# Kernel1's products with W, cut into stretches of 256 tokens

## The chip, the cores and the metric

The kernel runs on one core of one Trainium2 chip. The time is the device time of one execution in microseconds (us), and a kernel's time is the median over its runs. The core has five engines with instruction queues of their own: TensorE (PE in the profile; its weight loads are listed as PEld), VectorE (DVE), ScalarE (ACT), GpSimd (POOL) and SyncE (SP). Each works through its queue in order, and semaphores make one wait for another. The program has about 93,000 instructions, all laid out before it runs: there is no branch.

## The reference

Two layers over x, 16 batches of 1024 tokens by 256 features, all in float32. The first is a Nyström attention with 16 heads of 16 features and 64 landmarks:

```
Q = Q / sqrt(16)
Q_l, K_l = means of Q and K over groups of 16 tokens       # 64 landmarks
kernel1 = softmax(Q @ K_l^T)                               # tokens x landmarks
kernel2 = softmax(Q_l @ K_l^T)                             # landmarks x landmarks
kernel3 = softmax(Q_l @ K^T)                               # landmarks x tokens
SV  = (kernel1 @ iterative_inv(kernel2)) @ (kernel3 @ V)
out = SV @ w_proj
x   = x + layernorm(out)
```

iterative_inv is six steps of a Newton-like iteration with 64x64 matrices. The second layer normalizes x, computes for each batch the reconstruction loss of eight small experts, picks the expert with the least loss, and adds the layer norm of a base projection plus that expert's adapter.

## The kernel before, in words

**Four streams.** Each batch goes through four stages, and a Stream object runs each stage over all batches: a (norm, Q, K, V, kernel3 and its product with V, called u), p (kernel2 and its inverse, ending in W = inverse times u), c (kernel1, its product with W, the projection and the residual), and d1 with d2 (the experts). They are staggered: while d works on batch b, c works on b + 1, p on b + 2 and a on b + 3, roughly.

**The scheduler.** A stage is a generator. Before each step it yields `go(name, follows, parts)`: the step's name, the steps that must be over, and its parts: `mm(us, mode, n)` is TensorE work of estimated time us, in an array mode ("full", "r32", "c32", "q64"), of n instructions, and takes one PSUM slot; `ew(engine, us, behind, mark)` is work of another engine, where "free" gives a slot back. The loop at L1105 takes among the streams' next steps the one with the least key: for a step that starts on TensorE, the estimated idle time that it would put on TensorE (counted as zero up to 0.15 us), then the stream's progress less 0.1 if the step has the mode that TensorE is in; a step without TensorE goes first once its inputs are nearly there. The estimate in `tried` keeps a clock for each engine, four PSUM slots handed out in turn, 0.09 us for a change of mode, and instructions that arrive in blocks of 256, one every 3.4 us at most (BLOCK, FETCH; `run`). The order so chosen is the order of the instructions in every engine's queue.

**PSUM.** There is one pool, ps2, with four buffers of two banks each (L58). `two_banks` and `one_bank` are two names for the same allocation (L74 to L78): every tile, large or small, takes one of the four in turn, so a new tile waits until the tile allocated four places before it has been read.

**Stage c around the change.** A batch's tokens are handled in two windows n of 512. In each window, for each half c of the heads (8 heads, 4 pairs):

- `before_weights` and `weights` (L728): scores in transposed form, landmarks of a pair of heads on the partitions and 512 tokens along the row, less each token's maximum; two psct tiles; ScalarE takes the exponential into two e tiles (e1).
- the maxima of the next window (`max_of`, L686: two psc tiles, one VectorE reduction each), or in the last window the residual of the window before.
- `before_weighted` and `weighted` (L754): the product with W. The 512 tokens are four groups j of 128; for each j, each pair p and each group g of 32 tokens, 32 columns of e are the weights, and the 34 columns of w_bd (two heads by 16 features and a column of ones) stream through. These are 64 matmuls in the code and 128 in the profile, where a float32 matmul here is two; four run side by side, on four groups of 32 columns of the array. They fill a tile psv. The column of ones gives the softmax's denominators: VectorE takes their reciprocal (rec) and multiplies (svn).

After both halves of the heads, `turned_sv` (L779) transposes svn on TensorE (ptsv), ScalarE copies it (svt), and `projected` (L804) multiplies by w_proj (po).

The steps of other streams that appear below: ph and pr (experts' hidden layer and reconstruction, L879 and L911; VectorE evicts pr as df, L919, ScalarE squares it, L922), pq and pv (Q, K and V, L309 and L330), psm and psc of stage a (kernel3, L378 and L402), put (its product with V, L441), pm (transposed maxima, L723), rrow (a small step of the inverse's start, L584), and the inverse's 64x64 products, all at L533 (pkv, psq, pb, pvi).

Of the kernel before, what the change touches and what calls it, by code (L numbers as in the profile page):

```python
# [8 lines left out]
F32 = mybir.dt.float32  # L9
I32 = mybir.dt.int32  # L10
AF = mybir.ActivationFunctionType
ALU = mybir.AluOpType
# [3 lines left out]
P = 128  # L16
# [6 lines left out]
def kernel(  # L23
# [17 lines left out]
    nc = tc.nc  # L41
    NB, N, D = x.shape
    NT = N // P
    H, HD, M = 16, 16, 64
    G = N // M
    NC = D // P
    HC = H // NC
    NP = H // 2
    PC = NP // NC
    E, _, R = wa_down.shape  # L50
# [6 lines left out]
    small = ctx.enter_context(tc.tile_pool(name="small", bufs=2))  # L57
    ps2 = ctx.enter_context(tc.tile_pool(name="ps2", bufs=4, space=PSUM))  # L58

    def last(ap, n):  # L60

        return ap.unsqueeze(len(ap.shape)).to_broadcast([*ap.shape, n])
# [8 lines left out]
    def rows32(p):  # L71
        return slice(32 * p, 32 * p + 32)

    def two_banks(shape, name):  # L74
        return ps2.tile(shape, F32, tag="ps2", name=name)

    def one_bank(shape, name):
        return ps2.tile(shape, F32, tag="ps2", name=name)  # L78

    def buf4k(tag, shape, name, bufs=2):  # L80

        return work.tile(shape, F32, tag=tag, name=name, bufs=bufs)
# [70 lines left out]
    for c in range(NC):  # L153
        for r in range(2):
            j = 2 * c + r
# [49 lines left out]
    def mm(us, mode, n, bank="ps2"):  # L205
        return ("pe", us, mode, bank, n)

    def ew(engine, us, behind=-1, mark=""):
        return (engine, us, behind, mark)

    def go(name, follows, *parts):
        return name, follows, parts
# [457 lines left out]
    def stage_c(b):  # L670
# [5 lines left out]
        def before_max(n, t0):  # L676
            return go(
                ("c", b, "max", n, t0),
                first,
                mm(0.5, "r32", 32),  # L680
                mm(0.5, "r32", 32),
                ew("dve", 1.13, 1, "free"),
                ew("dve", 1.13, 1, "free"),
            )

        def max_of(n, t0):  # L686

            mx = maxima[n]
            psc = [two_banks([P, 2, 2, NC, P], f"psc1_{b}_{n}_{t0}_{g}") for g in range(PC // 2)]
            for c in range(NC):  # L690
                for t in range(2):
                    cols = slice((4 * n + t0 + t) * P, (4 * n + t0 + t + 1) * P)
                    for p in range(PC):
                        nc.tensor.matmul(  # L694
                            psc[p // 2][:, p % 2, t, c, :],
                            lhsT=qt[rows32(p), c, cols],
                            rhs=bd[rows32(p), NC + c, :, :].rearrange("f r l -> f (r l)"),
                            start=True,
                            stop=True,
                        )  # L700
            for g in range(PC // 2):
                nc.vector.tensor_reduce(  # L702
                    mx[:, t0 : t0 + 2, 64 * g : 64 * g + 64].rearrange("x t (p j) -> x p t j", p=2)[
                        :, :, :, 0 : 2 * NC
                    ],
                    psc[g].rearrange("x p t c (r l) -> x p t (c r) l", r=2),
                    X,
                    ALU.max,
                )

        def before_rows(n):
            return go(
                ("c", b, "mt", n),
                [("c", b, "max", n, t0) for t0 in range(0, 4, 2)],
                mm(0.44, "full", 8),
                ew("act", 0.5, -1, "free"),
            )
# [10 lines left out]
        def weights(n, c, mt):  # L728

            psc = [two_banks([P, 2, 512], f"psct_{b}_{n}_{c}_{g}") for g in range(PC // 2)]  # L730
            for p in range(PC):
                nc.tensor.matmul(  # L732
                    psc[p // 2][:, p % 2, :],
                    lhsT=bd[rows32(p), NC + c, :, :].rearrange("f r l -> f (r l)"),
                    rhs=qt[rows32(p), c, n * 512 : (n + 1) * 512],
                    start=True,
                    stop=False,
                )
            for p in range(PC):
                nc.tensor.matmul(  # L740
                    psc[p // 2][:, p % 2, :],
                    lhsT=minus_max[rows32(p), c, :, :].rearrange("f r l -> f (r l)"),
                    rhs=mt[rows32(p), :],
                    start=False,
                    stop=True,
                )
            es = []
            for g in range(PC // 2):
                e = buf4k("e1", [P, 2, 512], f"e1_{b}_{n}_{c}_{g}")
                nc.scalar.activation(e, psc[g], AF.Exp)  # L750
                es.append(e)
            return es

        def weighted(n, c, es, svn):  # L754

            psv = two_banks([P, 2, 512], f"psv_{b}_{n}_{c}")
            for j in range(4):
                for p in range(PC):
                    col = (j % 2) * PC * 2 * (HD + 1) + p * 2 * (HD + 1)
                    for g in range(4):  # L760
                        nc.tensor.matmul(  # L761
                            psv[rows32(g), j // 2, col : col + 2 * (HD + 1)],
                            lhsT=es[p // 2][:, p % 2, j * P + 32 * g : j * P + 32 * g + 32],
                            rhs=w_bd[:, c * PC + p].rearrange("x r d -> x (r d)"),
                            start=True,
                            stop=True,
                        )
            by_head = psv[:, :, 0 : 2 * H * (HD + 1) // 2].rearrange("x k (h d) -> x k h d", d=HD + 1)
            rec = small.tile([P, 2, H], F32, tag="rec", name=f"rec_{b}_{n}_{c}")
            nc.vector.reciprocal(rec, by_head[:, :, :, HD])  # L770
            for k in range(2):
                nc.vector.tensor_tensor(
                    svn[:, 2 * k : 2 * k + 2, c * P : (c + 1) * P].rearrange("x j (h d) -> x j h d", d=HD),
                    by_head[:, k, :, 0:HD].rearrange("x (j h) d -> x j h d", j=2),
                    last(rec[:, k, :], HD).rearrange("x (j h) d -> x j h d", j=2),
                    ALU.mult,
                )

        def turned_sv(n, svn):  # L779
            pt = two_banks([P, NC, 512], f"ptsv_{b}_{n}")  # L780
            for j in range(4):
                for c in range(NC):
                    nc.tensor.transpose(pt[:, c, j * P : (j + 1) * P], svn[:, j, c * P : (c + 1) * P], ident)
            nc.scalar.copy(svt[n], pt)  # L784

        def before_weights(n, c):
            return go(
                ("c", b, "e1", n, c),
                [("c", b, "mt", n)],
                mm(0.9, "r32", 16),  # L790
                mm(0.9, "r32", 16),
                ew("act", 0.93, 1, "free"),
                ew("act", 0.93, 1, "free"),
            )

        def before_weighted(n, c):
            return go(
                ("c", b, "sv", n, c),
                [("c", b, "e1", n, c), ("p", b, "end")],
                mm(1.15, "c32", 256),  # L800
                ew("dve", 0.95, -1, "free"),
            )

        def projected(n):  # L804
# [13 lines left out]
        def added(n, y, stats):  # L818
            res = live[b]["x1"][:, 4 * n : 4 * n + 4, :]
            yield from add_normalized(b, "c", n, y, stats, res, res)  # L820
# [10 lines left out]
        for n in range(NW):  # L831
            for c in range(NC):
                yield before_weights(n, c)
                es = weights(n, c, mt)
                if n + 1 < NW:
                    yield before_max(n + 1, 2 * c)
                    max_of(n + 1, 2 * c)
                elif c == 0:
                    yield from added(n - 1, *po)
                yield before_weighted(n, c)  # L840
                if c == 0:
                    svn = buf4k("yc", [P, 4, D], f"svn_{b}_{n}")
                weighted(n, c, es, svn)
            if n + 1 < NW:
                yield before_rows(n + 1)
                mt = max_rows(n + 1)
            yield go(
                ("c", b, "svt", n),
                [("c", b, "sv", n, c) for c in range(NC)],
                mm(0.88, "full", 16),  # L850
                ew("act", 0.93, -1, "free"),
            )
            svt[n] = work.tile([P, NC, 512], F32, tag="svt", name=f"svt_{b}_{n}", bufs=1)
            turned_sv(n, svn)
            po = yield from projected(n)
# [249 lines left out]
    with tc.manual_schedule(engines={mybir.EngineType.PE, mybir.EngineType.Activation, mybir.EngineType.DVE, mybir.EngineType.Pool}):  # L1105
        while any(s.takes for s in streams):
# [13 lines left out]
            _, s, at = best  # L1120
# [43 lines left out]
```

## Time and profile before

| what | value |
|---|---|
| median of 14 runs | 2582.27 us (2572.36 to 2592.65) |
| the profiled execution | 2588.31 us; span from first to last instruction 2586.5 us |
| mean granted TensorE clock in it | 0.961 |
| PE / PEld / DVE / ACT / POOL busy | 2310.1 / 1509.7 / 1544.0 / 1253.6 / 277.4 us |
| psv matmuls (L761) | 8192, 94.8 us busy |
| reciprocals (L770) | 64 of 128x32, 350 ns each |
| multiplications (L772) | 128 of 128x256, 420 ns each |

In the profile's lines, "out<-in" are the program's tile names, then the shapes as partitions x elements, then the count. In a group's line the numbers behind the bar are the busy time in us, the mean duration in ns and the idle time of the engine just ahead of these instructions, with what ended it. A line of the waits reads: who, for whom, us in total, times, the longest. "issue" means that the engine waited for nothing that the profile shows. The chain is the work that ended last, followed back from the last instruction.

### The profile page before, as it was taken

The numbers are of one execution on the slowest core, as the hardware profiler recorded it, in microseconds if no ns is written. First come the engines' busy times: TensorE is split into PE (matmuls) and PEld (weight loads), VectorE is DVE, ScalarE is ACT, GpSimd is POOL, SyncE is SP. The second block draws the span as 40 slices with busy tenths as digits, with TensorE's granted clock in tenths as the row PEclk, the third lists the DMA queues.
The fourth block names the chain that finished last, engine by engine and source line by source line (L and its number), as shares of the span: only waits on it lengthen the run. The fifth ranks groups of instructions, "written<-read, shape, count | busy, mean of one in ns | idle before, by whom it ended". The sixth has DMA issues, their size and how long they took to land.

```text
span 2586.5 us, 93024 instructions
## 1 busy us (share of the span) xinstructions
PE 2310.1 (89%) x42930; PEld 1509.7 (58%) x42930; DVE 1544.0 (60%) x3242; ACT 1253.6 (48%) x2147; POOL 277.4 (11%) x372
## 2 busy tenths in 40 slices
PE   6998988989999899898989899998998989998975
PEld 3666556565655656556565655656566565655543
DVE  5547465575666656665585665647566575664654
ACT  1344554545546355453645446354454645554534
POOL 1001011020100201011020111102011020101021
PEclk9899998999999999998999999999999999999978
DMA  3000001010010100101010010101001010100100
GB/s 102 19 19 3 18 5 51 2 38 18 4 51 3 47 9 13 42 5 51 2 38 18 18 37 5 38 15 38 18 5 51 2 37 2 37 3 4 34 19 19
DMA packets 56592, 60.81 MB, mean 24 GB/s; under 512 B 4949, under 2 KB 55178, under 8 KB 56202
## 3 DMA queue, kind: packets, MB, share of 16 engines
q1 hardware_dynamic: 50176, 50.34, 6.1%
q8 instruction: 337, 5.52, 0.9%
q0 software_dynamic: 2560, 2.14, 0.3%
q10 hardware_dynamic: 3466, 2.37, 0.3%
q14 instruction: 53, 0.43, 0.1%
HBM read 38.06 MB, written 16.78 MB: 21 GB/s over the span
## 4 chain that ended last, share of the span: by engine, by line
PE 60%; DVE 21%; ACT 9%; issue 3%; POOL 1%; DMA 0%; POOLq 0%; DVEq 0%; ACTq 0%
PE ph L879 8%; PE pq L309 8%; ACT df L922 5%; PE pf L1011 4%; PE pr L911 4%; PE po L809 4%; PE pv L330 3%; DVE df L919 3%; PE pkv L533 3%; PE pvi L533 3%; DVE maxima L702 3%; PE pf L1012 2%; PE psv L761 2%; PE psct L732 2%; DVE mx L387 2%
## 5 line engine op out<-in xcount | busy, mean ns | idle before, releaser
L922 ACT ACTIVATE df<-df,bd_sb 128x512 f32<-128x512 f32 x512 | 363.1, 711 | 244.5 <-DVE df L919 244.5
L919 DVE TENSOR_TENSOR df<-pr,xt_d 128x1024 f32<-128x1024 f32 x256 | 300.4, 1216 | 87.7 <-PE pr L911 56.1
L911 PE MATMUL pr<-ht,wd_sb 64*128 64x512 f32 x1024 | 259.0, 619 | 9.6 <-ACT ht L887 4.6
L879 PE MATMUL ph<-xt_d,wd_sb 128*128 128x512 f32 x512 | 236.8, 606 | 3.7 <-DVE df L919 3.6
L309 PE MATMUL pq<-xt_a,wqkv_sb 128*128 128x512 f32 x512 | 234.0, 604 | 4.1 <-DVE df L919 1.7
L423 ACT ACTIVATE e<-psc 128x1024 f32<-128x1024 f32 x128 | 123.1, 1024 | 123.4 <-PE psc L413 123.2
L750 ACT ACTIVATE e<-psct 128x1024 f32<-128x1024 f32 x128 | 123.6, 1017 | 118.9 <-PE psct L740 116.8
L702 DVE TENSOR_REDUCE maxima<-psc 128x16 f32<-128x1024 f32 x128 | 150.4, 1218 | 47.7 <-PE psc L694 47.5
L387 DVE TENSOR_REDUCE mx<-psm 128x2 f32<-128x1024 f32 x128 | 149.2, 1217 | 25.2 <-PE psm L378 25.1
L309 PEld LDWEIGHTS pq<-xt_a,wqkv_sb 128*128 128x128 f32 x512 | 95.8, 192 | 115.1 <-issue 106.6
L879 PEld LDWEIGHTS ph<-xt_d,wd_sb 128*128 128x128 f32 x512 | 92.7, 191 | 115.9 <-issue 93.7
L222 POOL TENSOR_SCALAR ve_c_y<-mv_c_y 128x4 f32<-128x4 f32 x32 | 10.1, 314 | 1364.7 <-DVE mv_c_y L220 1290.9
L911 PEld LDWEIGHTS pr<-ht,wd_sb 64*128 64x128 f32 x1024 | 86.5, 186 | 100.5 <-issue 58.7
L219 DVE BATCH_NORM_STATS2 st_c_y<-y_c 128x6 f32<-128x256 f32 x128 | 51.4, 401 | 147.4 <-ACT y_c L264 147.4
L533 PEld LDWEIGHTS pkv<-vi,k2t 64*64 64x64 f32 x6144 | 103.0, 139 | 61.9 <-issue 21.7
L1011 PE MATMUL pf<-wbase_sb,xt_d 128*128 128x256 f32 x512 | 136.2, 389 | 0.0
L219 DVE BATCH_NORM_STATS2 st_d_y<-y_d 128x6 f32<-128x256 f32 x128 | 51.5, 402 | 140.0 <-ACT y_d L264 140.0
L533 PE MATMUL pkv<-vi,k2t 64*64 64x64 f32 x6144 | 116.9, 226 | 18.4 <-ACT vi L653 6.9
L317 DVE TENSOR_REDUCE lsum<-qt 128x64 f32<-128x1024 f32 x32 | 39.0, 1220 | 143.8 <-ACT qt L316 143.8
L761 PE MATMUL psv<-w_bd,e 128*32 128x34 f32 x8192 | 94.8, 201 | 31.8 <-issue 19.3
L809 PE MATMUL po<-wproj_sb,svt 128*128 128x256 f32 x512 | 119.4, 387 | 2.5 <-ACT svt L784 2.5
L609 ACT COPY kvs<-pkv 128x1024 f32<-128x1024 f32 x96 | 96.7, 1007 | 48.8 <-PE pkv L533 26.6
(175 smaller groups left out, 4302.8 us busy)
## 6 DMA issues: line engine op xcount, KB each, us to landing
xa<-in_L_attn_x_dram SPq DMA_DIRECT2D x16, 1024.0 KB, 5.4
x<-in_L_attn_x_dram SPq DMA_DIRECT2D x16, 1024.0 KB, 7.3
out_dram<-y_d SPq DMA_DIRECT2D x32, 512.0 KB, 3.0
wqkv_sb<-in_L_attn_w_qkv_dram ACTq DMA_DIRECT2D x1, 768.0 KB, 6.2
wd_sb<-in_L_ffn_Wd_dram ACTq DMA_DIRECT2D x2, 256.0 KB, 12.6
wd_sb<-in_L_ffn_Wd_dram ACTq DMA_DIRECT2D x1, 512.0 KB, 14.3
wdn<-in_L_ffn_Wa_down_dram,row POOLq DMA_INDIRECT x32, 2.5
wproj_sb<-in_L_attn_w_proj_dram ACTq DMA_DIRECT2D x1, 256.0 KB
```

What stands on the lines that cost most here:

```text
L309: nc.tensor.matmul(pq[:, n, :], lhsT=wqkv_sb[:, k, f0 : f0 + P], rhs=xt[:, k, n * 512 : (n + 1) * 512], start=(k == 0), stop=(k == NC - 1),)
L387: nc.vector.tensor_reduce(mx3[:, n, q : q + 2], psc[g], X, ALU.max)
L533: nc.tensor.matmul(dst[64 * h[to] : 64 * h[to] + 64, 4 * h[frm] + 2 * g0 + g1, :], lhsT=x[rows, i, :], rhs=y[rows, j, :] if y_at else y[ro ...
L702: nc.vector.tensor_reduce(mx[:, t0 : t0 + 2, 64 * g : 64 * g + 64].rearrange("x t (p j) -> x p t j", p=2)[:, :, :, 0 : 2 * NC], psc[g].rea ...
L750: nc.scalar.activation(e, psc[g], AF.Exp)
L761: nc.tensor.matmul(psv[rows32(g), j // 2, col : col + 2 * (HD + 1)], lhsT=es[p // 2][:, p % 2, j * P + 32 * g : j * P + 32 * g + 32], rhs= ...
L809: nc.tensor.matmul(po[:, j, :], lhsT=svt[n][:, c, j * P : (j + 1) * P], rhs=wproj_sb[:, c, :], start=(c == 0), stop=(c == NC - 1),)
L879: nc.tensor.matmul(ph[:, n, :], lhsT=wd1_sb[:, k, 2 * i : 2 * i + 2, :].rearrange("p e h -> p (e h)"), rhs=xt[:, k, n * 512 : (n + 1) * 51 ...
L911: nc.tensor.matmul(pr[:, r, :], lhsT=wd2_sb[half, i, k * P : (k + 1) * P], rhs=ht[half, cols], start=True, stop=True,)
L919: nc.vector.tensor_tensor(df, pr, middle(xt[:, k, cols], 2), ALU.subtract)
L922: nc.scalar.activation(df[:, r, :], df[:, r, :], AF.Square, bias=bd2_sb[:, e, k : k + 1], accum_out=part[:, e, k * NW + n : k * NW + n + 1],)
L1011: nc.tensor.matmul(po[:, j, :], lhsT=xt[:, k, cols], rhs=wbase_sb[:, k, :], start=(k == 0), stop=False)
```

## The change

The product with W of one (n, c) becomes two, k = 0 and k = 1, each over two of the four groups of 128 tokens. Each half has a tile psv of its own (2 x 4 x 34 float32 a partition, in one bank, but one slot of the pool), a reciprocal of its own with half the elements, and one multiplication, as each k had before. Each half is a step of its own for the scheduler, with half the TensorE estimate (0.58 us, 128 instructions) and 0.6 us of VectorE in place of 0.95. `turned_sv` waits for all four halves of its window.

```diff
-        def weighted(n, c, es, svn):
-            psv = two_banks([P, 2, 512], f"psv_{b}_{n}_{c}")
-            for j in range(4):
+        def weighted(n, c, es, svn, k):
+            psv = one_bank([P, 2, PC, 2 * (HD + 1)], f"psv_{b}_{n}_{c}_{k}")
+            for j in range(2):
                 for p in range(PC):
-                    col = (j % 2) * PC * 2 * (HD + 1) + p * 2 * (HD + 1)
                     for g in range(4):
+                        t0 = (2 * k + j) * P + 32 * g
                         nc.tensor.matmul(
-                            psv[rows32(g), j // 2, col : col + 2 * (HD + 1)],
-                            lhsT=es[p // 2][:, p % 2, j * P + 32 * g : j * P + 32 * g + 32],
+                            psv[rows32(g), j, p, :],
+                            lhsT=es[p // 2][:, p % 2, t0 : t0 + 32],
                             rhs=w_bd[:, c * PC + p].rearrange("x r d -> x (r d)"),
                             start=True,
                             stop=True,
                         )
-            by_head = psv[:, :, 0 : 2 * H * (HD + 1) // 2].rearrange("x k (h d) -> x k h d", d=HD + 1)
-            rec = small.tile([P, 2, H], F32, tag="rec", name=f"rec_{b}_{n}_{c}")
+            by_head = psv.rearrange("x j p (r d) -> x j (p r) d", r=2)
+            rec = small.tile([P, 2, HC], F32, tag="rec", name=f"rec_{b}_{n}_{c}_{k}")
             nc.vector.reciprocal(rec, by_head[:, :, :, HD])
-            for k in range(2):
-                nc.vector.tensor_tensor(
-                    svn[:, 2 * k : 2 * k + 2, c * P : (c + 1) * P].rearrange("x j (h d) -> x j h d", d=HD),
-                    by_head[:, k, :, 0:HD].rearrange("x (j h) d -> x j h d", j=2),
-                    last(rec[:, k, :], HD).rearrange("x (j h) d -> x j h d", j=2),
-                    ALU.mult,
-                )
+            nc.vector.tensor_tensor(
+                svn[:, 2 * k : 2 * k + 2, c * P : (c + 1) * P].rearrange("x j (h d) -> x j h d", d=HD),
+                by_head[:, :, :, 0:HD],
+                last(rec, HD),
+                ALU.mult,
+            )
...
-        def before_weighted(n, c):
+        def before_weighted(n, c, k):
             return go(
-                ("c", b, "sv", n, c),
+                ("c", b, "sv", n, c, k),
                 [("c", b, "e1", n, c), ("p", b, "end")],
-                mm(1.15, "c32", 256),
-                ew("dve", 0.95, -1, "free"),
+                mm(0.58, "c32", 128),
+                ew("dve", 0.6, -1, "free"),
             )
...
-                yield before_weighted(n, c)
-                if c == 0:
-                    svn = buf4k("yc", [P, 4, D], f"svn_{b}_{n}")
-                weighted(n, c, es, svn)
+                for k in range(2):
+                    yield before_weighted(n, c, k)
+                    if (c, k) == (0, 0):
+                        svn = buf4k("yc", [P, 4, D], f"svn_{b}_{n}")
+                    weighted(n, c, es, svn, k)
...
                 ("c", b, "svt", n),
-                [("c", b, "sv", n, c) for c in range(NC)],
+                [("c", b, "sv", n, c, k) for c in range(NC) for k in range(2)],
```

## The prediction

> **What bounds the kernel now.** First the page: the span, the engines' shares, and the chain that ended last.
>
> ```profile
> span 2586.5 us, 93024 instructions
> PE 2310.1 (89%) x42930; PEld 1509.7 (58%) x42930; DVE 1544.0 (60%) x3242; ACT 1253.6 (48%) x2147; POOL 277.4 (11%) x372
> q8 instruction: 337, 5.52, 0.9%
> PE 60%; DVE 21%; ACT 9%; issue 3%; POOL 1%; DMA 0%; POOLq 0%; DVEq 0%; ACTq 0%
> ```
>
> TensorE is the bound: 89% busy and 60% of the chain. It is idle for about 276 us, and an edit that adds no matmul can only change those. The q8 line will matter: 5.52 MB of instructions came in 337 packets, 16 KB each; over 2 x 42930 TensorE instructions that is one packet per 256.
>
> Second, the groups and waits of the tile that the change cuts in two.
>
> ```profile
> L761 PE MATMUL psv<-w_bd,e x8192: 191/197/267, 186.2 to 2475.4; 128*32 128x34 f32 x200
> L772 DVE TENSOR_TENSOR svn<-psv,rec x128: 414/420/426, 189.0 to 2476.4; 128x256 f32<-128x256 f32 x128
> L770 DVE RECIPROCAL rec<-psv x64: 338/350/358, 188.6 to 2475.7; 128x32 f32<-128x32 f32 x64
> L492 DVE RECIPROCAL rs<-pu 128x8 f32<-128x8 f32 x16 | 3.3, 207 | 16.7 <-PE pu L487 16.7
> PE psv L761 <- issue: 19.3, 20, 1.7
> PE ptsv L783 <- DVE svn L772: 5.9, 6, 3.2
> DVE rec L770 <- PE psv L761: 18.9, 11, 5.5
> ```
>
> 8192 matmuls are 64 products of 128 (four run side by side, so a product takes 1.30 us undisturbed: 94.8 us busy in all). After it VectorE runs 350 + 2 x 420 ns = 1.19 us. Two waits stand out: 19.3 us inside the products in which TensorE waited for nothing shown ("issue"), and few waits (5.9 us) of the transposes of svn behind the division.
>
> Third, the timeline of TensorE and VectorE at one product, with the four evictions ahead of it (start, length, work).
>
> ```profile
> 638.96 1.30 PE L761 MATMUL psv<-w_bd,e 128*32 128x34 f32 x128
> 640.19 0.66 PE L723 MATMUL pm<-ident,maxima 128*128 128x128 f32 x4
> 641.22 3.70 PE L879 MATMUL ph<-xt_d,wd_sb 128*128 128x512 f32 x8 [0.37 <-DVE df L919]
> ...
> 637.69 4.61 DVE L919 TENSOR_TENSOR df<-pr,xt_d 128x1024 f32<-128x1024 f32 x4
> 642.22 0.35 DVE L770 RECIPROCAL rec<-psv 128x32 f32<-128x32 f32 x1
> 642.60 0.76 DVE L772 TENSOR_TENSOR svn<-psv,rec 128x256 f32<-128x256 f32 x2
> ```
>
> This is the resource that the change takes more of. PSUM is one pool of four slots (tag "ps2"), handed out in turn: each new tile waits until the tile four places earlier is evicted. Here four pr tiles fill the slots, and VectorE frees one every 1.13 us (at about 638.9, 640.0, 641.2, 642.3). psv takes the first, pm the second, ph the third, and ph waits for it (the 0.37 us "<-DVE df").
>
> Fourth, a stall of "issue" from close by:
>
> ```profile
> 707.35 0.69 PE L533 MATMUL pvi<-t,vt 64*64 64x64 f32 x32
> 707.87 0.65 PE L533 MATMUL pvi<-vt,t 64*64 64x64 f32 x32
> 708.44 1.02 PE L761 MATMUL psv<-w_bd,e 128*32 128x34 f32 x94
> 711.07 0.48 PE L761 MATMUL psv<-w_bd,e 128*32 128x34 f32 x34 [1.61 <-issue]
> ```
>
> Short products of the inverse (128 instructions in about 1.1 us) run straight into psv's 256 (matmuls and weight loads), and in the middle TensorE stands for 1.61 us: the next packet of instructions is not there yet.
>
> **The change, part by part.** Sums are against the profiled execution, 2588.31 us (span 2586.5), which lies 6.0 us above the median of 2582.27.
>
> *Matmuls.* Number, shapes and operands stay: 64 x 128 becomes 128 x 64. Zero.
>
> *Reciprocals.* 64 of 128x32 (350 ns) become 128 of 128x16. Between 207 ns (128x8) and 350 ns (128x32) the line gives 6 ns an element and 255 ns for 16. So 64 x (2 x 255 - 350) = +10.2 us of VectorE. Its cover is VectorE's 40% idle time; where the chain runs on VectorE (21%) there is none: +2.1 us; ends 0 and 10.2. The multiplications stay 128 at 420 ns.
> The line's fixed part is 159 ns an instruction. [...]
>
> *PSUM slots.* The one term with weight. one_bank and two_banks draw on the same pool and tag, so each half takes a whole slot: 64 more allocations for the same TensorE work, and every tile after a product waits for an eviction one place later. At 638.96: the second half would like to start at 639.61 and gets its slot at 640.04 (+0.43); pm then needs the slot of 641.17 instead of 640.04 and starts 1.0 us later than it did; ph needs that of 642.30, 1.1 us later. Waiting at the head of TensorE's queue, the half holds up all four batches' work behind it. I did this for all 64 products, with the ends of the evictions three, two and one places before it: the second half would be late at 28 of them, 13.7 us in sum; the tile after it at 24, 17.4 us; the larger of these two at each product sums to 23.6 us, and with the second tile after it 39.3 us. What gives some back: the halves are divided and freed after 0.68 us each, where the whole held its slot through 1.19 us, and in a stretch that VectorE bounds, TensorE would have waited a little later anyway. I take 23.6 x 0.6, TensorE's share of the chain: +14.2 us; ends 0 (all absorbed) and 39.3.
>
> *The tail.* After the last matmul VectorE has 255 + 420 = 0.68 us to do in place of 1.19. svn's readers waited on it 13 times (14.3 us over matmuls and weight loads): at most 13 x 0.51 = -6.7 us; the transposes themselves show only 6 matmul waits: -3.0 us taken; the other end 0. Late next is ACT's copy of ptsv, which follows as before. In other places the first division, queued earlier, waits in front of VectorE's next eviction, as the whole did (18.9 us, 11 times).
>
> *Instruction packets.* The scheduler now chooses between the halves, so long matmuls can stand there while a packet arrives: between -19.3 us (all of psv's issue waits) and +5.5 us (the same wait at put, L441, whose steps of 64 matmuls are as short as the halves will be). But it leaves the halves only when the next one's estimated wait is over 0.15 us and another stream's is less, or another stream is behind by more than its bonus of 0.1 for staying in the same mode; and a late slot holds every candidate alike. So mostly they will stand next to each other. A quarter: -5 us.
> The row says that the queue stalls TensorE by 33 us (psv 19.3, put 5.5, pkv 3.9, pb 2.9, pvi 1.8). [...]
>
> *The order.* Every later choice of the scheduler can turn out otherwise. The bound is in the trace: the first product of one batch starts 144.5 to 160.4 us after that of the batch before (batches 2 to 14), for the same work in different orders; standard deviation 4.5 us. Over 14 batches that is 6.4 us if a late one gives back at the next (4.5 x root 2), and 16.8 us if all are independent. I take 0 +- 12 us. DMA queues (SP, POOL's gathers) get nothing added, but the gathers follow d's order.
>
> Sum: 2.1 + 14.2 - 3.0 - 5.0 = +8.3 us: 2596.6 us against the profiled execution, **2590 us** as a median.
>
> **The rivals.** *Faster: the choice breaks the stalls.* Half products fit beside long matmuls, the issue waits in psv go, and the slots cost nothing since halves leave early: 2582.3 - 19.3 - 6.7 + 2.1 = 2558 at best, 2568 with slots at +10. For: 20 stalls of up to 1.7 us. Against: packets hold 256 instructions and arrive no faster; many stalls lie where the work before psv was dense, and then a first half stalls too. It decides once psv's issue waits fall under some 6 us (13 us gained against the 8.3 of the forecast and the 0.2% bound).
> *No change:* the halves stay together and the slot waits fall where TensorE would have waited for the same evictions: 2.1 - 3 = 2581. For: the runs of 1.13 us evictions show VectorE as the bound just there. Against: after most products a step of 3.4 us or more follows soon, with no wait of its own to absorb it.
> *Much slower:* slots at the upper end, 39.3, less tail and packets, +10 of order: about 2610. It needs the scheduler to put steps of one slot and little work (rrow, mt) behind the halves.
>
> **How the numbers follow.** About 0.2% (5.2 us) is what a measurement of this kernel can tell from no change. Forecast 0.50 (own range 2583 to 2606; 0.03 of it within the bound), faster rival 0.25, no change 0.15, much slower 0.10: faster 0.25, same 0.18, slower 0.57. The spread: slots +-12, order +-12, packets +-8, VectorE and tail +-4, together about 19 us, times 1.28: **2566 to 2614**.
>
> **What would show it.** psv in 128 groups of 64 matmuls at 0.65 us, 128 reciprocals near 255 ns, VectorE busy up by 10 us. Slots: more waits of psv, pm, ph, pr and pv on VectorE's df, maxima and mx (psv's own matmuls wait 6.1 us for these now). Packets: psv's issue wait 14 us or so. Tail: ptsv's wait on svn down by half. The prediction is wrong if other tiles' slot waits don't grow, if the halves are mostly apart with psv's issue wait near nothing, or if the new order moves whole batches by more than 12 us.

## The result, and the profile after

The kernel with half products takes 2606.33 us (median of 10 runs, 2594.63 to 2608.99), the kernel before 2579.95 us (47 runs). The ratio is 1.0096 (95% interval 1.0077 to 1.0116): 25 us slower, between 20 and 30. The forecast was 2590 us, +8.3.

The profiled execution of the changed kernel took 2598.69 us, less than its median, where that of the kernel before (2588.31) lay above its own. So the two traces differ by only 10.4 us of span, and no single line of them can be expected to show all 25. Comparisons between kernels below rest on the runs, and the traces tell where the time went. "Us" worked out of a ratio is (ratio - 1) x 2580.

The page of the changed kernel, with the lines that answer to the first view of before:

```profile
span 2596.9 us, 93066 instructions
PE 2315.8 (89%) x42930; PEld 1517.3 (58%) x42930; DVE 1556.3 (60%) x3306; ACT 1253.1 (48%) x2147; POOL 283.2 (11%) x372
q8 instruction: 337, 5.52, 0.9%
PE 57%; DVE 23%; ACT 11%; issue 3%; POOL 1%; DMA 0%; POOLq 0%; DVEq 0%; ACTq 0%
```

TensorE has the same 42930 matmuls. VectorE has 64 more instructions and 12.3 us more to do. In the chain, TensorE lost 3 points, and VectorE and ScalarE gained 2 each: TensorE waits for evictions more often.

The tile that was cut, in the changed kernel (shortest, median and longest duration, in ns):

```profile
L761 PE MATMUL psv<-w_bd,e x8192: 191/197/265, 183.1 to 2492.8; 128*32 128x34 f32 x200
L770 DVE RECIPROCAL rec<-psv x128: 236/249/259, 185.4 to 2493.1; 128x16 f32<-128x16 f32 x128
L771 DVE TENSOR_TENSOR svn<-psv,rec x128: 423/425/426, 185.7 to 2493.4; 128x256 f32<-128x256 f32 x128
```

The shapes are those of the diff: 128 reciprocals of 249 ns, 128 multiplications of 425 ns. Now the waits of the changed kernel (who, for whom, us in total, times, the longest):

```profile
PE psc L402 <- DVE svn L771: 37.9, 8, 6.1
...
PE put L441 <- issue: 11.9, 8, 2.9
PE psv L761 <- issue: 8.9, 8, 2.3
...
PE psv L761 <- DVE mx L387: 4.0, 18, 0.7
...
PE ptsv L782 <- DVE svn L771: 1.0, 1, 1.0
```

The first line is new: in the kernel before, psc (a score tile of stage a) waited for maxima and mrow, never for svn. It is the largest of TensorE's waits in this trace: 8 times, 4.7 us each. The lines with "issue" are those that the prediction put down to instruction packets: psv's wait fell from 19.3 to 8.9 us, but that of put rose from 5.5 to 11.9.

One of the eight, in the timeline of TensorE and VectorE (start, length, work, and in brackets the idle time before it and what ended it):

```profile
1170.15 1.09 PE L761 MATMUL psv<-w_bd,e 128*32 128x34 f32 x92
...
1171.65 0.48 PE L761 MATMUL psv<-w_bd,e 128*32 128x34 f32 x35 [0.41 <-issue]
...
1173.00 1.13 PE L402 MATMUL psc<-mrow,ones 32*128 32x512 f32 x4
...
1173.53 0.39 DVE L219 BATCH_NORM_STATS2 st_a<-xa 128x6 f32<-128x256 f32 x1
...
1178.47 0.69 DVE L628 SCALAR_TENSOR_TENSOR t<-kvs,eye 128x512 f32<-128x512 f32 x1
1179.07 0.25 DVE L770 RECIPROCAL rec<-psv 128x16 f32<-128x16 f32 x1
1179.36 0.42 DVE L771 TENSOR_TENSOR svn<-psv,rec 128x256 f32<-128x256 f32 x1
1179.70 0.25 DVE L770 RECIPROCAL rec<-psv 128x16 f32<-128x16 f32 x1
1179.93 1.23 PE L402 MATMUL psc<-mrow,ones 32*128 32x512 f32 x2 [5.80 <-DVE svn L771]
1179.98 0.42 DVE L771 TENSOR_TENSOR svn<-psv,rec 128x256 f32<-128x256 f32 x1
```

Both halves of a batch's last product are over at 1172.1. Their divisions stand in VectorE's queue behind the statistics of two normalizations (24 instructions, from 1171.4 to 1178.0) and two steps of the inverse, and the first starts 7 us later. Until then the halves hold two of the four slots, where the whole held one. TensorE gets four more psc matmuls in, and the next psc waits 5.80 us for the first half's slot.

What such a wait does afterwards is seen in the windows of the same kernel (stretch, its length, busy time of PE, PEld, DVE, ACT and POOL, then the granted clock of TensorE and what the DMAs did):

```profile
1174.20:1177.60 3.40, 0.00 (x0) 0.00 (x0) 3.16 (x13) 0.00 (x0) 2.11 (x3) 1.00 1.01 311
1177.60:1181.00 3.40, 1.07 (x12) 1.06 (x14) 3.30 (x11) 0.00 (x0) 1.90 (x2) 0.50 0.03 10
1181.00:1184.40 3.40, 3.40 (x58) 2.69 (x56) 1.99 (x7) 0.98 (x2) 0.00 (x0) 0.50 0.02 5
1184.40:1187.80 3.40, 3.40 (x72) 2.95 (x67) 0.69 (x1) 1.97 (x3) 0.00 (x0) 0.50 0.00 0
1187.80:1191.20 3.40, 3.40 (x132) 2.73 (x124) 0.42 (x1) 0.87 (x1) 0.00 (x0) 0.99 0.02 5
```

TensorE stands from 1174.1 to 1179.9, and runs at half clock from 1177.6 to 1187.8. It works through 58 and 72 matmuls in two stretches there. So the wait costs 5.8 us and then, as an estimate, some 4 us more: half of the 7.9 us of work done at half clock.

### The profile page after: what moved, and what is told of

The parts are those of the page before. It is cut to its first block, busy times and chain, and to the rows that moved or that the text cites. A ratio compares the mean times of both kernels' runs of the same rounds, so it can differ in the third digit from the quotient of the medians.

```text
span 2596.9 us, 93066 instructions
## 1 busy us (share of the span) xinstructions
PE 2315.8 (89%) x42930; PEld 1517.3 (58%) x42930; DVE 1556.3 (60%) x3306; ACT 1253.1 (48%) x2147; POOL 283.2 (11%) x372
## 4 chain that ended last, share of the span: by engine, by line
PE 57%; DVE 23%; ACT 11%; issue 3%; POOL 1%; DMA 0%; POOLq 0%; DVEq 0%; ACTq 0%
PE ph L879 8%; PE pq L309 8%; ACT df L922 6%; PE pf L1011 4%; PE po L808 4%; PE pr L911 4%; DVE maxima L702 4%; PE pv L330 3%; PE pvi L533 3%; DVE df L919 2%; PE pkv L533 2%; DVE mx L387 2%; PE pf L1012 2%; PE psct L732 2%; PE pb L533 1%
## 5 line engine op out<-in xcount | busy, mean ns | idle before, releaser
L911 PE MATMUL pr<-ht,wd_sb 64*128 64x512 f32 x1024 | 259.5, 622 | 10.2 <-ACT e L750 3.6
L222 POOL TENSOR_SCALAR ve_c_y<-mv_c_y 128x4 f32<-128x4 f32 x32 | 10.2, 319 | 1406.2 <-DVE mv_c_y L220 1406.2
L402 PE MATMUL psc<-mrow,ones 32*128 32x512 f32 x512 | 96.6, 693 | 42.5 <-DVE svn L771 37.9
L761 PE MATMUL psv<-w_bd,e 128*32 128x34 f32 x8192 | 104.1, 200 | 23.7 <-issue 8.9
L330 PE MATMUL pv<-wqkv_sb,xt_a 128*128 128x256 f32 x512 | 118.0, 384 | 0.1
## 6 DMA issues: line engine op xcount, KB each, us to landing
wd_sb<-in_L_ffn_Wd_dram ACTq DMA_DIRECT2D x1, 512.0 KB, 14.2
```

The source lines that it names most:

```text
L330: nc.tensor.matmul(pv[:, j, :], lhsT=xt[:, k, (t0 + j) * P : (t0 + j + 1) * P], rhs=wqkv_sb[:, k, 2 * D : 3 * D], start=(k == 0), stop=(k ...
L911: nc.tensor.matmul(pr[:, r, :], lhsT=wd2_sb[half, i, k * P : (k + 1) * P], rhs=ht[half, cols], start=True, stop=True,)
```

## The experiments

The theory: a half takes a whole slot (one of the four buffers of the PSUM pool), so 64 more slots are taken for the same work, and that costs the time. The rivals: the second reciprocal; the scheduler's new order, whatever the slots; and the granted clock. Each run lists its mean granted clock, and that matters here: over the 82 runs of the kernel before, the clock lay between 0.958 and 0.971, the time between 2567 and 2592 us, and they go together (correlation -0.85, 1.7 us less for each 0.001 of clock). A fit over all kernels' runs, with one slope and one offset for each kernel, gives the last column: the difference to the kernel before at the same clock (a single run lies 2.9 us beside the fit, so these are good to about 3 us). That the slope within a kernel also holds between kernels is assumed. And where a kernel's own waits lower its clock, this column takes out a part of what that kernel costs: it is no better than the ratio, only another reading.

| kernel | ratio, 95% interval | us by the ratio | mean clock | us at equal clock |
|---|---|---|---|---|
| the changed kernel | 1.0096 (1.0077 to 1.0116) | +25 | 0.9584 | +11.5 |
| halves_old_order | 1.0108 (1.0074 to 1.0142) | +28 | 0.9637 | +24.4 |
| one_slot_two_recs | 1.0024 (0.9999 to 1.0048) | +6 | 0.9646 | +3.2 |
| one_slot_new_order | 1.0022 (1.0004 to 1.0040) | +6 | 0.9629 | -1.3 |
| after_sooner | 1.0058 (1.0033 to 1.0083) | +15 | 0.9629 | +8.6 |
| sooner_one_slot | 1.0026 (1.0003 to 1.0049) | +7 | 0.9600 | -2.6 |
| halves_c0 | 1.0089 (1.0054 to 1.0123) | +23 | 0.9618 | +15.2 |
| touched_slot | 1.0157 (1.0131 to 1.0183) | +41 | 0.9632 | +37.3 |
| empty_slot | 1.0005 (0.9982 to 1.0029) | +1 | 0.9645 | 0.0 |
| shared_slot | 1.0004 (0.9980 to 1.0027) | +1 | 0.9642 | -1.8 |
| order_1p16 | 1.0084 (1.0054 to 1.0114) | +22 | 0.9614 | +15.7 |
| later_whole | 1.0077 (1.0053 to 1.0102) | +20 | 0.9589 | +8.0 |
| sooner_whole | 1.0033 (1.0013 to 1.0053) | +8 | 0.9605 | +1.7 |

The kernel before has a mean clock of 0.9657.

**halves_old_order: the slots without the new order.** The changed kernel, but both halves of a product are one step again, with the old estimates. Every other step stands exactly where it stood before.

```diff
-                mm(0.58, "c32", 128),
-                ew("dve", 0.6, -1, "free"),
+                mm(1.15, "c32", 256),
+                ew("dve", 0.95, -1, "free"),
...
+                yield before_weighted(n, c)
                 for k in range(2):
-                    yield before_weighted(n, c, k)
```

> The two halves of each product with a slot, a reciprocal and a multiplication of their own, but as one step for the scheduler with the old estimates, so that every other instruction stands where it stood before the change. Slots theory (that of the prediction: the 64 extra slots hold TensorE up): 9 to 26 us over the kernel before, some 13 (14.2 slots + 2.1 reciprocals - 3 tail). Order theory (the loss comes from where the scheduler now puts the last product of a batch: behind VectorE's normalizations): within 6 us of the kernel before, and no wait of psc (L402) on svn over 1 us.

**one_slot_two_recs: the reciprocals without the slots.** The kernel before, with a reciprocal for each k. It has the instruction list and the order of halves_old_order, and one tile for a product in place of two.

```diff
-            nc.vector.reciprocal(rec, by_head[:, :, :, HD])
             for k in range(2):
+                nc.vector.reciprocal(rec[:, k, :], by_head[:, k, :, HD])
```

> The kernel before, order and slots as they were, with the one reciprocal of 32 elements made two of 16, each followed by its multiplication. Both theories: the price of the reciprocals alone, +2 us (0 to +10); VectorE busy +9 us. If the reciprocals carry the loss instead: +20 us or more.

The first lost 28 us, more than was expected, the second 6 (the interval begins just under 0). They differ in the slots alone: 22 us, 11 to 32 by the two intervals, 21 at equal clock. With the order held, the slots alone cost as much as the whole change. The timeline of halves_old_order at the place that the prediction worked out:

```profile
630.62 4.61 DVE L919 TENSOR_TENSOR df<-pr,xt_d 128x1024 f32<-128x1024 f32 x4
...
631.89 0.77 PE L761 MATMUL psv<-w_bd,e 128*32 128x34 f32 x64
...
633.02 0.77 PE L761 MATMUL psv<-w_bd,e 128*32 128x34 f32 x64 [0.36 <-DVE df L919]
...
634.15 0.66 PE L723 MATMUL pm<-ident,maxima 128*128 128x128 f32 x4 [0.37 <-DVE df L919]
...
635.28 3.70 PE L879 MATMUL ph<-xt_d,wd_sb 128*128 128x512 f32 x8 [0.47 <-DVE df L919]
```

Each step starts on one of VectorE's evictions, 1.13 us apart. In the kernel before, pm came 1.23 us after the start of the product, here 2.26: +1.03, where +1.0 was predicted; ph came 2.26 us after it, here 3.39: +1.13, predicted +1.1. The second half is late by 0.48 us, predicted +0.43.

The two traces have the same steps in the same order, so the time from each step's start to the next can be compared step by step. Against the kernel before, halves_old_order spends 12.5 us more in the products, 18.5 more in the step after, 3.7 in the second after, 4.5 less in the third, and 11.3 less in all the rest; 13.3 us of that last saving is a matter of half clock falling elsewhere. Without what half clock adds or takes (taken as half of each half-clock stretch), it is 10.9 in the product and 13.6 in the step behind it: 24.5 us.

A part of it need not be listed as a wait. Groups of halves_old_order (busy us and mean ns behind the bar, then idle time before):

```profile
L761 PE MATMUL psv<-w_bd,e 128*32 128x34 f32 x8192 | 100.6, 202 | 32.3 <-issue 11.7 <-DVE df L919 5.8 <-DVE mx L387 5.2
...
L732 PE MATMUL psct<-qt,bd 32*128 32x512 f32 x512 | 93.1, 674 | 3.8 <-DVE mx L387 0.9 <-DVE df L919 0.8 <-DVE t L634 0.8
...
L740 PE MATMUL psct<-mt,minus_max 32*128 32x512 f32 x512 | 83.9, 612 | 0.0
```

The psct matmuls take 93.1 and 83.9 us; in the kernel before they take 85.6 and 77.3, and in one_slot_two_recs 85.0 and 76.6. A psct step fills two slots, and starts as soon as it has the first. One such step of halves_old_order, where the second came late:

```profile
464.84 1.13 PE L732 MATMUL psct<-qt,bd 32*128 32x512 f32 x4
466.57 0.70 PE L732 MATMUL psct<-qt,bd 32*128 32x512 f32 x2 [0.61 <-DVE k L566]
```

The second tile's first matmul starts 1.73 us after the step does, and only 0.61 us of that is listed as a wait; in a step with both slots free it starts within 0.02 us. This happens in 17 of the 64 steps (16.8 us in sum), and in the kernel before in 10 (8.1 us). The two groups overlap in such a step, so their times can't be added: from their first start to their last end the 64 steps take 152.0 us against 142.6, and of these 9.4 us some 3 are half clock by the same estimate.

**one_slot_new_order: the new order without the slots.** The changed kernel's steps, estimates and order of choices, but both halves fill one tile, and the division follows the second.

```diff
-            psv = one_bank([P, 2, PC, 2 * (HD + 1)], f"psv_{b}_{n}_{c}_{k}")
+            if k == 0:
+                both[c] = two_banks([P, 2, 512], f"psv_{b}_{n}_{c}")
+            psv = both[c][:, k, 0 : 4 * PC * (HD + 1)].rearrange("x (j p e) -> x j p e", j=2, p=PC)
...
+            if k == 0:
+                return
```

> The changed kernel's order of steps to the instruction, but both halves write one tile (one slot), with one reciprocal and two multiplications after the second half, as before the change. Slots theory: back to within 8 us of the kernel before, since no slot and no reciprocal is added. Order theory: 15 to 28 us over the kernel before, like the changed kernel, with psc (L402) still waiting 3 to 6 us for a slot in the batches in the middle.

It lost 6 us (1 to 10), none at equal clock. The changed kernel is 19 us slower than it (12 to 26 by the intervals), 13 at equal clock. They differ in the slots and also in the second reciprocals, which took 6 us with the order held, or 3 at equal clock; that leaves some 13 us for the slots, or 10. Its waits:

```profile
PE pb L533 <- DVE svn L777: 30.4, 8, 4.5
...
PE psv L764 <- issue: 12.9, 14, 1.7
```

So the new order alone puts the last product behind the normalizations, and a step waits for its slot; but with one slot held in place of two, TensorE gets further first and waits at most 4.5 us, later, at pb. The late eviction comes from the order, and the slots make it dearer: 37.9 us of waits where these are 30.4. Behind the eight waits the changed kernel has 78 us at half clock, and this one some 51 at the same eight places; but over the whole traces it is 199 and 205 us, so how much of the 19 us this makes is not shown.

**after_sooner: halves, but ahead of the normalizations.** The scheduler's key prefers the products by 0.15 of a batch. **sooner_one_slot** is the same with one tile, as in one_slot_new_order.

```diff
-                    key = (wait if wait > 0.15 else 0.0, s.progress() - same)
+                    sooner = 0.15 if s.takes[0][2] == "sv" else 0.0
+                    key = (wait if wait > 0.15 else 0.0, s.progress() - same - sooner)
```

> The changed kernel, where the scheduler counts a stream's progress as 0.15 less while its next step is one of these products, so that the products of the last heads go ahead of stage a's weights and of VectorE's normalizations in all 16 batches. Slots theory: as slow as the changed kernel, 15 us or more over the kernel before, since all 64 extra slots and reciprocals stay. Order theory: the waits of psc (L402) on svn go, and most of the loss with them: within 10 us of the kernel before.

> The order of the kernel with the 0.15 preference (the last product ahead of the normalizations in all batches), to the step, but both halves write one tile with one reciprocal, as before the change. Slots theory: about 20 us under that kernel with two slots (which took +14), so -10 to 0 us against the kernel before. If slots cost nothing in this order: +10 to +18 like that kernel.

15 and 7 us slower than before; at equal clock the second is 3 faster. In after_sooner psc no longer waits for svn, but 15 us of loss stay. That sooner_one_slot would be as fast as the kernel before or faster was missed by the ratio. The difference of the two, what slots and second reciprocals cost in a third order, is 8 us (-1 to 17), 11 at equal clock. So the slots took 22 us alone in the first order, and 19 and 8 us together with the reciprocals in the other two (21, 13 and 11 at equal clock). The intervals overlap: that the price depends on the order around them is likely, and not shown.

**halves_c0: half as many extra slots.** halves_old_order, but only the products of the first eight heads are halved (32 extra slots in place of 64), with the whole product kept for c = 1:

```diff
                 if c == 0:
                     svn = buf4k("yc", [P, 4, D], f"svn_{b}_{n}")
-                weighted(n, c, es, svn)
+                    for k in range(2):
+                        weighted(n, c, es, svn, k)
+                else:
+                    whole(n, c, es, svn)
```

> The old order again, with a slot and a reciprocal of its own for each half, but only in the first half of the heads (c = 0): 32 extra slots in place of 64. Slots theory: the price goes by the number of slots that fall into stretches of evictions, +10 to +20 us (halves of all products: +29). If one place of a batch carries the loss (the last product, c = 1, in front of the normalizations): within 5 us of the kernel before.

It lost 23 us (14 to 32), or 15 at equal clock. Half of the 28 us of halves_old_order would be 14, half of its 24 at equal clock 12. So it may be more than half, which would mean that it matters which steps stand behind a slot, but the runs don't show that it is.

**touched_slot: an extra slot without halves.** The kernel before with its whole product and its order. Ahead of each product a tile of its own gets one product of 32x2, which VectorE copies out after the division; the result is thrown away.

```diff
+            extra = two_banks([P, 2, 512], f"extra_{b}_{n}_{c}")
+            nc.tensor.matmul(
+                extra[0:32, 0, 0:2], lhsT=es[0][:, 0, 0:32], rhs=w_bd[:, c * PC, 0, 0:2], start=True, stop=True
+            )
...
+            junk = small.tile([32, 2], F32, tag="junk", name=f"junk_{b}_{n}_{c}")
+            nc.vector.tensor_copy(junk, extra[0:32, 0, 0:2])
```

> What the run with an empty tile was meant to be. A tile that is never used gets no slot (its 1793 tiles lay at the addresses of the kernel before), so here the second tile beside each whole psv is used as little as can be: one product of 32x2, and a VectorE copy of it after the multiplications (64 more VectorE instructions, about as much time as the split reciprocals add). Whole products, old order, 64 extra slots: 1857 tiles, as many as the changed kernel has. Slots theory: +12 to +28 us over the kernel before (halves with slots of their own at this order: +28; the same halves in one slot: +5). If a slot is cheap and the break in the product is what costs: 0 to +8 us.

It lost 41 us (34 to 47), the most of all and more than was expected, with nearly no work added for TensorE. Its psv group:

```profile
L765 PE MATMUL psv<-w_bd,e 128*32 128x34 f32 x8192 | 95.7, 202 | 37.7 <-issue 11.5 <-DVE mx L387 9.5 <-DVE df L925 7.7
```

Here the second slot is held until the whole product is divided, where the first half is freed early. That it costs more than the halves fits the slots; half products and second reciprocals are not there to explain it (VectorE is busy 1548.5 us, between before and the changed kernel). What the 64 small products and copies cost apart from their slot was not measured.

**empty_slot: an extra slot that nothing uses.** This run missed its purpose.

```diff
             psv = two_banks([P, 2, 512], f"psv_{b}_{n}_{c}")
+            two_banks([P, 2, 512], f"unused_{b}_{n}_{c}")
```

> The kernel before, instruction for instruction in the old order, with whole products; beside each psv a second tile of the pool is named and never written or read. It adds no work; it only makes every later tile wait for an eviction one place nearer. Slots theory: most of what halves at the old order cost, +12 to +22 us over the kernel before (halves at the old order took +29, halves in one slot +7). If the halves cost through something else (their reciprocals, a break in the product, semaphores): within 5 us of the kernel before.

No loss, 1.0005. The unused tiles got no buffer: all 1793 tiles have the addresses that they had before, so this is the kernel before once more. It shows how far apart two equal kernels measure (0.05%), and nothing about slots; touched_slot was made in its place.

**shared_slot: fewer slots.** The inverse's first product (pvt) and the second (psq of its first step) share a tile, 16 allocations less.

```diff
+            psq = pvt = banks_of(f"psq{i}")
...
-                pvt = banks_of("pvt")
...
-            psq = banks_of(f"psq{i}")
```

> The kernel before with slots saved, not added: in the first step of the inverse, the transposes pvt and the product psq, which each fill one half of a tile, share one tile. 16 fewer allocations, the old order of instructions. Slots theory: at 0.35 us a slot (22 us for 64), 0 to 6 us faster than the kernel before. Against it: the shared slot is held until both evictions are done.

1.0004: no gain that can be measured (-0.2% to +0.3%, or -5 to +7 us, where 0 to 6 us of gain were expected). Whether slots at this place are worth less, or the longer hold of the shared one took the gain back, isn't shown.

**order_1p16, later_whole, sooner_whole: other orders of the whole product.** The kernel before with 0.01 us more in one estimate, with the products 0.3 of a batch later in the key, and with them 0.06 sooner.

```diff
-                mm(1.15, "c32", 256),
+                mm(1.16, "c32", 256),
```

> The kernel before with one number of the scheduler changed: the product's TensorE estimate is 1.16 us (twice 0.58, as the change has it) in place of 1.15. Whole products, 64 slots, 64 reciprocals; but the steps come in another order, and the last product of a batch stands behind VectorE's normalizations in eight or nine of the 16 batches (before: in two or three). Order theory: +4 to +15 us over the kernel before, with a lower granted clock. Slots theory alone: within 5 us.

```diff
-                    key = (wait if wait > 0.15 else 0.0, s.progress() - same)
+                    sooner = -0.3 if s.takes[0][2] == "sv" else 0.0
+                    key = (wait if wait > 0.15 else 0.0, s.progress() - same - sooner)
```

> The kernel before with whole products and the scheduler counting a stream as 0.3 further while its next step is such a product: the last product of a batch now stands behind VectorE's normalizations in 11 of 16 batches. If that place is what costs in an order: +10 to +30 us, waits of stage a's steps on svn of 2 to 6 us in most batches, granted clock 0.958 or so. If the place does not matter: within 6 us of the kernel before.

In sooner_whole the line reads `sooner = 0.06 if ...`.

> The kernel before with whole products and a preference of 0.06 for them: the last product goes ahead of the normalizations in 13 of 16 batches and behind one of their steps in three; nothing else is changed. If that place is what costs in an order: 0 to 8 us faster than the kernel before, which has it in one batch fully and four in part. If an order's time is a lottery over many waits: anything between -10 and +20 us.

All three lost: 22, 20 and 8 us (of the first, 4 to 15 were expected). 0.01 us in an estimate is worth 0.84% (0.54 to 1.14): about as much as the whole change. Part of it goes with the clock (0.9614, 0.9589, 0.9605); 16, 8 and 2 us remain at equal clock. In the trace of later_whole the last product's division stands behind 24 statistics instructions in 10 of 16 batches, and its waits show the same picture with one slot:

```profile
PE pb L533 <- DVE svn L772: 26.0, 8, 4.9
```

But that place alone doesn't set an order's price: one_slot_new_order has it in 8 batches and lost 6 us, none at equal clock. What else makes an order dear isn't shown. That sooner_whole would be faster was a miss. All five other orders with one slot for a product measured slower by the ratio (6 to 22 us), but at equal clock three of them stay within 3 us, and none of the twelve experiments beat the kernel before.

## Why the prediction was right, and where its size was wrong

The sign, the range (2566 to 2614) and the mechanism were right: the change makes the kernel slower, and the largest part of that by the ratio, some 13 us, comes because a half takes a whole slot. The size was off by 17 us, the median lies just above the forecast's own range (2583 to 2606), and most of the waits stand at other places than those that were counted. By the runs, the 17 us divide so: slots, reciprocals and tail together cost 19 us where 13.3 were taken, order and packets 6 (one_slot_new_order) where -5 were, each good to 5 to 7 us. At equal clock they are 13 and -1, close to what was taken, and the clock has the rest.

*Slots.* The step that was off is "I take 23.6 x 0.6, TensorE's share of the chain: +14.2 us". With the order held, the sum of the places without the discount, 23.6 us, fits better: the runs give 22 us, 21 at equal clock, and the traces 24.5 us in the product and the step behind it (the interval of the runs, 11 to 32, has 14.2 in it too). The chain's share of 60% says how often TensorE is the bound over the whole span; these places are TensorE's own, and the step waits at the head of its queue. What was thought to give some back (the halves leave early, VectorE would bound there anyway) didn't show with the order held. The single place at 638.96 came out to within 0.05 us on all three steps.

In the new order the slots took some 13 us (10 at equal clock), close to the discounted 14.2. That is luck: the places are others. The prediction said that it would be wrong if other tiles' slot waits didn't grow, and named psv, pm, ph, pr and pv waiting for df, maxima and mx. In sum these waits are 19.1 us before, 27.2 in halves_old_order, and 19.0 in the changed kernel (though 53 times in place of 36). What grew there is psc's wait for svn, from nothing to 37.9 us.

*Where a division stands in VectorE's queue.* The prediction took the division as coming right after the product, as at 638.96. In the changed kernel's trace, 24 statistics instructions of VectorE stand ahead of the last product's division in 8 of 16 batches, and it starts some 8 us after the first half is done. In the kernel before at most 8 do, in one batch, and it starts within 3.2 us. That the halves hold two slots for that long, 7 to 8 us and not 0.7, was no term of the sum. The term for it was "order, 0 +- 12". This change's own order, with one tile for both halves (one_slot_new_order), cost 6 us, within these bounds; but order_1p16 and later_whole, with 22 and 20 us, show that the bounds were too narrow for an order that isn't known.

*Reciprocals.* Right. 249 ns where 255 was estimated, VectorE busy +12.3 us where +10.2 was: the reciprocals alone give +9.6, and the rest comes from the multiplications, which no longer follow each other in pairs (two in a row take 0.76 us, one alone 0.42). In time it was +6 us by the ratio (0 to 12), 3 at equal clock, where 2.1 was taken. 350 ns for 32 elements and 249 for 16 leave a fixed part of 148 ns an instruction, where the prediction's line has 159.

*Tail.* ptsv's wait on svn fell from 5.9 to 1.0 us: -4.9, where -3.0 was taken.

*Packets.* Taken -5: psv's issue waits fell by 10.4 us, to 8.9 (14 predicted), and put's rose by 6.4. Net -4. That these waits are packets fits the kernel before, behind the stall that the prediction shows:

```profile
711.07 0.48 PE L761 MATMUL psv<-w_bd,e 128*32 128x34 f32 x34 [1.61 <-issue]
711.48 1.16 PE L533 MATMUL pkv<-vi,k2t 64*64 64x64 f32 x64
712.57 0.65 PE L441 MATMUL put<-e,v_ones 128*32 128x64 f32 x30
714.54 0.72 PE L441 MATMUL put<-e,v_ones 128*32 128x64 f32 x34 [1.32 <-issue]
```

From one stall to the next there are 34 + 64 + 30 matmuls, with their weight loads 256 instructions: one packet, in 3.5 us. Over the whole trace only 38 such waits of TensorE (in psv, put, pkv, pb and pvi) stand against 337 packets; in this dense stretch two of them come one packet apart.

*The clock.* It was no term at all: the prediction held that an edit without new matmuls can only change TensorE's 276 us of idle time. In the traces the granted clock is 0.961 before and 0.962 after, but over all runs 0.9657 and 0.9584. By the slope of 1.7 us for 0.001, some 13 of the 25 us go with the clock; 11.5 are left at equal clock. That the waits of psc lower it is argued, not shown: in the trace seven of the eight come with 10.2 us at half clock, as above, and the eighth with 6.8 us, but the kernel before has half-clock stretches of its own (205 us in its trace, 199 in that of the changed kernel), and the profiled execution of the changed kernel is one of its faster ones. With the order held the clock has little part: halves_old_order keeps 24 of its 28 us at equal clock. How the 25 us divide between slots, order and clock is therefore open, by up to these 13 us. That only 6 are left when the halves share one slot and one reciprocal is not.

*The rivals.* The faster one needed psv's issue waits under 6 us; they fell to 8.9, and put took up most of the gain. No change needed the slot waits to fall where TensorE would have waited anyway; with the order held they don't. The much slower one was put at about 2610, and the 2606 measured lies nearer to that than to 2590; but its cause, 39.3 us of slots, didn't come, and its own terms with the forecast's tail and packets (39.3 + 2.1 - 3 - 5 + 10) would give 2626. Its price was possible: touched_slot, with the extra slot held to the end, lost 41.

## What to carry to other kernels

Where a pool has few buffers and hands them out by the tile, cutting a step in two doubles what it takes, whatever the size of the pieces: count the allocations, work out the waits at every place, and have a reason for each place before you discount what stands at the head of the bounding engine's queue. Look also at what is queued ahead of the eviction on its engine: a tile held for 7 us behind a normalization made TensorE wait 5.8 us, where its own division takes 0.7. Before crediting or blaming an edit to a scheduled kernel, measure what a trivial change of order is worth, and compare the granted clocks: here one such change was worth 22 us, and up to 13 of the 25 us went with the clock.

## What the runs showed of the hardware

- In the traces of the kernel before and of the changed kernel the clock is granted as full or half (1.00 or 0.50), and the 30 and 28 half-clock stretches are 3.4 us long or multiples of it (6.8, 10.2, 13.7, 17.1), but for the last one of each (10.7 and 11.6 us). After a wait of 5.8 us in the changed kernel it stayed at half for 10.2 us, 1177.6 to 1187.8, though TensorE was busy from 1179.9 on: 1181.0 to 1184.4 and 1184.4 to 1187.8, both fully busy (3.40 of 3.40 us), passed before the full clock came back.
- The 82 runs of the kernel before differ by 25 us (1%), and their mean clock goes from 0.958 to 0.971: 1.7 us less for each 0.001 (correlation -0.85).
- The late second buffer of a step that starts on the first need not show as a wait: in the step at 464.84 us of halves_old_order 1.73 us passed, and 0.61 are listed. Such late starts sum to 16.8 us there, and to 8.1 in the kernel before.
- Two of TensorE's "issue" waits come a packet apart in a dense stretch of the kernel before: 256 instructions and 3.5 us from the one that ends at 711.07 us (1.61 us long) to the one that ends at 714.54 (1.32 us). That they are waits for instructions is inferred from this distance.
